# A four-layer graph network on one core: after each gather of the GpSimd queue, 300 bytes of a row of its own are set to zero

## The chip, the cores and the metric

The kernel runs on one core of a Trainium2 chip. The metric is the time on the device in microseconds, the median of several runs; a profiled execution gives the rows that are read below. The five engines have an instruction queue each: TensorE (PE), VectorE (DVE), ScalarE (ACT), GpSimd (POOL) and SyncE (SP). SP does no arithmetic here, it starts DMAs. POOL starts the indirect ones, in which a list of row numbers says which rows of a table in device memory are fetched (a gather) or written (a scatter).

## What is computed

2708 nodes with 128 features each, and a sparse weighted adjacency matrix `adj` of 2708 x 2708 (about 17 entries to a row, the diagonal among them). Four layers follow each other, each `x = layernorm(x + layer(x))`:

```python
x = _layernorm(x + _L0_gnn_ref(x, adj))   # (adj.T @ x) / column sums of adj
x = _layernorm(x + _L1_gnn_ref(x, adj, ...))
#   messages = gelu(s[i] + d[j] + b); aggregated[i] = sum_j adj[i, j] * messages[i, j]
#   h = gelu([x, aggregated] @ upd_w.T + upd_b) + x, then a layernorm with weights
x = _layernorm(x + _L2_gnn_ref(x, adj, ...))
#   adj @ (x @ W) + b, normalised over all nodes, leaky relu
x = _layernorm(x + _L3_gnn_ref(x, adj, ...))
#   4 attention heads: s = exp(8 tanh(leaky_relu(x1[i] + x2[j]) @ a / 8)) * adj, rows normalised,
#   out = leaky_relu(s @ x @ Wlin.T), heads joined by w
```

## The kernel before

The nodes lie in 22 blocks of 128 rows (the last has 20).

**Layer 0 and the search.** SP loads `adj` block by block into a ring of nine buffers (`rows`). For each block PE multiplies it into the sums of layer 0 (L420). POOL clears the block's diagonal in place (`clear_diagonal`, L410); ACT then counts the entries of each row (L431). DVE searches each row for its entries (`extract`: L445, L450, L458 to L488) and keeps up to 32 columns and weights a row. Nodes are ranked by their number of entries (`ranking`), and `place` writes each node's list to its place in a sorted table, `lists_dram`, by scatters of POOL (L255). `layer0` then normalises the sums four blocks at a time (L790, into `dx` or `late`), transposes them, makes `d` of layer 1 from them, has SP store it to `d_dram` (L813), and scatters the rows to `dx_dram` (`own_scatter`). The tile `dx` has two buffers. The search of blocks 13 to 21 and their transposes come after the last L790 by a stated order (`behind`).

**Layer 1.** For each block of 128 sorted nodes `messages` gathers, slot by slot, the row of `d_dram` of the neighbour in that slot: 128 rows of 512 bytes by one indirect DMA of POOL. The slots go in groups of up to eight into one of five buffers `msg`; DVE adds the block's own term to the group (L896), ACT takes the gelu (L899), and DVE weighs each slot into a sum (L882, L884). `update` finishes the block and scatters its rows to `x2_dram`. Meanwhile PE, ACT and SP transpose `adj` into `at_dram` (L969, L974, L976), the first blocks loaded once more.

**Layer 2.** `layer2(k)` gathers the rows of `at_dram` in sorted order into the ring and multiplies (L1018); it begins while layer 1 still runs. Its normalisation follows, with the tables for layer 3.

**Layer 3.** 100 groups of four gathers each from `t2_dram` (`fetch`, into nine buffers `g`), then products on DVE, sums on ACT, and PE.

**What sets the order.** A scheduler that works with modelled durations orders each engine's instructions when the kernel is built, and takes what is ready; in the search and `layer0` the order of DVE is that of the text, and in layer 3 that of PE, DVE and ACT. POOL's order is the scheduler's throughout. Each engine works its queue in order: an instruction that waits holds up all behind it. POOL's queue holds the diagonal clears, all scatters and all gathers. For a tile that is written again the scheduler adds a wait of the later write for the earlier, on POOL itself too.

`gather` is the helper by which layers 1, 2 and 3 fetch rows: 368, 22 and 400 times.

Of the kernel before, what the change touches and what calls it, by code (L numbers as in the profile page):

```python
# [28 lines left out]
I8 = mybir.dt.int8  # L29
# [56 lines left out]
def gnn_resnorm_kernel(  # L86
# [21 lines left out]
    nc = tc.nc  # L108
# [98 lines left out]
    keep = ctx.enter_context(tc.tile_pool(name="keep", bufs=1))  # L207
# [31 lines left out]
    ones = keep.tile([P, P], FP, name="ones")  # L239
    nc.gpsimd.memset(ones, 1.0)  # L240

    def natural(dram, b0, b1):

        return dram[b0 * P : b1 * P, :].rearrange("(b p) w -> p b w", p=P)

    def gather(dst, table, index):
        nc.gpsimd.indirect_dma_start(  # L247
            out=dst,
            out_offset=None,
            in_=table[0:N, :],  # L250
            in_offset=bass.IndirectOffsetOnAxis(ap=index, axis=0),
        )

    def scatter(table, index, rows):
        return nc.gpsimd.indirect_dma_start(  # L255
            out=table,
            out_offset=bass.IndirectOffsetOnAxis(ap=index, axis=0),
            in_=rows,
            in_offset=None,
        ).ins  # L260
# [76 lines left out]
    with ExitStack() as layer:  # L337
# [527 lines left out]
        def messages(b, x_s, three):  # L865
# [24 lines left out]
            for c0, c1 in chunks_of(kk):  # L890
                kc = c1 - c0
                msg = msgs.tile([P, 8, D], FP, name="msg")
                for k in range(kc):
                    gather(msg[0:n, k, :], d_dram, idx[0:n, b, c0 + k + 1 : c0 + k + 2])
                mk = msg[0:n, 0:kc, :]
                nc.vector.tensor_tensor(  # L896
                    mk, mk, s_ps[0:n].unsqueeze(1).to_broadcast((n, kc, D)), ALU.add
                )
                nc.scalar.activation(mk, mk, AF.Gelu)  # L899
                for k in range(kc):  # L900
                    weigh(c0 + k + 1, msg[0:n, k, :])
# [99 lines left out]
        def layer2(k):  # L1001

            b, n = TURNS[k], BLOCKS[TURNS[k]][1]
            at = ring.tile([P, N], FP, name="at_rows", tag="rows")
            gather(at[0:n, :], at_dram, perm[0:n, b : b + 1])
            weighed = small.tile([P, P], FP, name="weighed", bufs=1)
            nc.scalar.activation(
                weighed[0:n], ones[0:n], AF.Copy, scale=column_sum[0:n, b : b + 1]
            )
            for ib in range(NBLK) if k == 0 else ORDER:  # L1010
                i0, m = BLOCKS[ib]
                if ib == 21:

                    nc.tensor.matmul(
                        accs2[5][:, 2 * D : 3 * D], lhsT=weighed[0:n], rhs=xw[0:n, b, :],
                        start=False, stop=False,
                    )
                nc.tensor.matmul(  # L1018
                    accs2[ib // 4][0:m, (ib % 4) * D : (ib % 4 + 1) * D],
                    lhsT=at[0:n, i0 : i0 + m],  # L1020
                    rhs=xw[0:n, b, :],
                    start=(k == 0 and ib % 4 == 0),
                    stop=(k == NBLK - 1 and ib in (3, 7, 11, 15, 19, 20)),
                )
# [73 lines left out]
    with ExitStack() as layer:  # L1098
        work = layer.enter_context(tc.tile_pool(name="bn", bufs=1))
        small = layer.enter_context(tc.tile_pool(name="bn_small", bufs=2))  # L1100
        hb = work.tile([P, NBLK, D], FP, name="hb")
        x2 = work.tile([P, NBLK, D], FP, name="x2")
        nc.sync.dma_start(x2[:, 0:NFULL, :], natural(x2_dram, 0, NFULL))
        nc.sync.dma_start(x2[0:NREM, NFULL, :], x2_dram[NFULL * P : N, :])
        a_all = keep.tile([P, HEADS, D], FP, name="a_all")
# [133 lines left out]
    with ExitStack() as layer:  # L1239
# [290 lines left out]
        def fetch(i):  # L1530
            b, j = quads[i]
            e = BLOCKS3[b][0] * (P // BLOCKS3[b][0])
            g4 = got.tile([P, 4, RW], FP, name="g4")
            for r in range(4):
                ch = CHUNK3[b] + 4 * j + r
                gather(g4[0:e, r, :], t2_dram, idx3[0:e, ch : ch + 1])
            gathered[i] = g4
# [559 lines left out]
```

## Time and profile before

| | |
|---|---|
| three runs, us | 1930.35, 1936.67, 1926.28; median 1930.35 |
| the profiled execution, span | 1936.7 us |
| busy: PE, DVE | 1240.9 us (64%), 1166.6 us (60%) |
| busy: POOL, ACT | 892.8 us (46%), 776.5 us (40%) |
| POOL's gathers of layer 1 (`msg`) | 368, mean 947 ns |
| POOL's gathers of layer 3 (`g`) | 400, mean 996 ns |
| DMA issued by POOL (queue 0) | 190.77 MB in 60496 packets |
| granted clock of PE, mean | 0.667 |

The span is the time from the first to the last instruction of that one execution. A line of the views below names a line of the kernel, the engine, the operation, the tile written and the tiles read, the shapes and how often; then come times. In a view in order of time the first two numbers are the start and the duration in us, and a bracket at the end gives how long the engine was idle before the instruction, and what ended that. In a view of groups the numbers after the bar are the busy time in us, the mean of one in ns, and the idle time before them. "issue" and "remote" stand where the profile names no instruction of another engine that ended the wait. SPq is SP's queue of DMA issues.

### The profile page before, as it was taken

How to read it: one execution, taken by the hardware profiler on the slowest of the kernel's cores; microseconds unless marked ns; L12 is line 12 of the kernel's file. 1: busy time of each engine (PE TensorE's matmuls, PEld its weight loads, DVE VectorE, ACT ScalarE, POOL GpSimd, SP SyncE). 2: the span in 40 equal slices, each digit the busy share in tenths (PEclk: the TensorE clock that was granted, in tenths of full speed). 3: DMA queues.
4: the chain of work that ended last, by engine and by line, in shares of the span. 5: the costliest groups of instructions: out<-in, count | busy, mean ns of one | idle time of the engine just before them, and what ended most of it. 6: DMA issues, size and time to landing. Idle time of an engine off the chain costs nothing. (4 is left out here: it accounts for less than half of the span.)

```text
span 1936.7 us, 23643 instructions
## 1 busy us (share of the span) xinstructions
PE 1240.9 (64%) x5771; PEld 864.1 (45%) x5771; DVE 1166.6 (60%) x4895; ACT 776.5 (40%) x3156; POOL 892.8 (46%) x1003
## 2 busy tenths in 40 slices
PE   7974313353446553554673748888788788878885
PEld 7973212242334442554663314544444444444444
DVE  8997445675635423433447417777678677676774
ACT  3565345543324210211122415555455555445553
POOL 1004654445653366445331474655555556555430
PEclk9986555555555576776676756676676777666675
DMA  8642645666545525223231574865566655756540
GB/s 283 238 150 79 131 140 165 174 183 174 141 103 142 177 43 160 95 92 140 79 113 44 167 239 131 212 190 163 145 196 183 182 166 160 191 150 192 150 115 7
DMA packets 167676, 289.63 MB, mean 150 GB/s; under 512 B 49600, under 2 KB 121502, under 8 KB 160429
## 3 DMA queue, kind: packets, MB, share of 16 engines
q0 software_dynamic: 60496, 190.77, 34.4%
q1 hardware_dynamic: 99489, 92.57, 15.6%
q10 hardware_dynamic: 7544, 4.69, 1.0%
q8 instruction: 48, 0.79, 0.2%
q14 instruction: 99, 0.81, 0.1%
HBM read 242.51 MB, written 45.36 MB: 149 GB/s over the span
## 5 line engine op out<-in xcount | busy, mean ns | idle before, releaser
L247 POOL DMA_INDIRECT g<-t_dram,idx x400 | 398.6, 996 | 316.0 <-issue 178.9
L247 POOL DMA_INDIRECT msg<-d_dram,idx x368 | 348.6, 947 | 260.2 <-issue 164.8
L1389 ACT ACTIVATE sum_junk<-g 126x128 bf16<-126x128 f32 (+3 forms) x1024 | 301.3, 296 | 142.4 <-issue 59.8
L1358 PE MATMUL z<-x,copies 32*126 32x512 f32 (+3 forms) x800 | 221.3, 944 | 65.8 <-DVE g L1555 45.0
L969 PE MATMUL pt_a<-ident,rows 128*128 128x128 f32 (+2 forms) x475 | 114.1, 395 | 144.4 <-ACT at_sb L974 79.5
L1555 DVE TENSOR_TENSOR g<-g,z 126x1536 f32<-126x1536 f32 (+3 forms) x100 | 175.0, 1750 | 44.0 <-DMA g<-t_dram,idx 15.3
L1018 PE MATMUL acc<-x_nat,at_rows 128*128 128x128 f32 (+2 forms) x968 | 160.7, 326 | 52.3 <-DMA at_rows<-at_dram,perm 26.5
L1389 ACT ACTIVATION_READ_ACCUMULATOR sum_junk<-g 126x1 f32 (+3 forms) x1024 | 191.6, 187 | 0.0
L1018 PEld LDWEIGHTS acc<-x_nat,at_rows 128*128 128x128 f32 (+2 forms) x968 | 144.1, 232 | 65.5 <-issue 38.7
L1363 PE MATMUL z<-g,ident 126*126 126x512 f32 (+3 forms) x200 | 169.3, 941 | 0.7 <-issue 0.7
L1435 PE MATMUL po_s<-wm,g 126*128 126x24 f32 (+6 forms) x800 | 128.6, 316 | 58.5 <-DVE wm L1422 56.2
L1435 PEld LDWEIGHTS po_s<-wm,g 126*128 126x128 f32 (+3 forms) x800 | 124.8, 243 | 75.6 <-DVE wm L1422 67.9
L969 PEld LDWEIGHTS pt_a<-ident,rows 128*128 128x128 f32 (+2 forms) x475 | 82.9, 205 | 167.5 <-ACT at_sb L974 92.8
L884 DVE SCALAR_TENSOR_TENSOR own<-msg,ls,own 128x128 f32<-128x128 f32 (+1 forms) x302 | 105.6, 350 | 85.4 <-ACT msg L899 28.5
L1381 DVE SCALAR_TENSOR_TENSOR g<-g,a_ps 126x1536 f32<-126x1536 f32 (+6 forms) x100 | 151.0, 1510 | 0.0
L420 PE MATMUL acc<-x_nat,rows 128*128 128x129 f32 (+3 forms) x1012 | 128.5, 288 | 26.0 <-DMA rows<-in_adj_dram 14.9
L420 PEld LDWEIGHTS acc<-x_nat,rows 128*128 128x128 f32 (+2 forms) x1012 | 123.0, 198 | 31.2 <-DMA rows<-in_adj_dram 16.0
L1358 PEld LDWEIGHTS z<-x,copies 32*126 32x126 f32 (+3 forms) x800 | 67.8, 261 | 100.3 <-issue 46.5
L899 ACT ACTIVATE msg<-msg 128x896 f32<-128x896 f32 (+4 forms) x55 | 50.4, 917 | 132.9 <-DVE msg L896 92.1
L1373 DVE SCALAR_TENSOR_TENSOR g<-z,a 126x128 f32<-126x128 f32 (+3 forms) x400 | 91.9, 285 | 19.5 <-remote 9.2
L445 DVE FIND_INDEX8 ci<-cv,rows 128x8 uint32<-128x247 f32 (+2 forms) x242 | 98.7, 408 | 0.0
L1363 PEld LDWEIGHTS z<-g,ident 126*126 126x126 f32 (+3 forms) x200 | 42.0, 263 | 124.3 <-issue 117.3
(302 smaller groups left out, 2132.2 us busy)
## 6 DMA issues: line engine op xcount, KB each, us to landing
rows<-in_adj_dram SPq DMA_DIRECT2D x34, 1354.0 KB
at_dram<-at_sb SPq DMA_DIRECT2D x105, 256.0 KB
g<-t_dram,idx POOLq DMA_INDIRECT x400
msg<-d_dram,idx POOLq DMA_INDIRECT x368
t_dram<-t_row SPq DMA_DIRECT2D x21, 256.0 KB
x_s<-dx_dram SPq DMA_DIRECT2D x21, 128.0 KB
at_dram<-at_sb SPq DMA_DIRECT2D x21, 64.0 KB
t_dram<-x_nat SPq DMA_DIRECT2D x5, 256.0 KB
```

The costliest lines, as they stand in the source:

```text
L247: nc.gpsimd.indirect_dma_start(out=dst, out_offset=None, in_=table[0:N, :], in_offset=bass.IndirectOffsetOnAxis(ap=index, axis=0),)
L420: nc.tensor.matmul(accs0[k][0:m, c0 : c0 + f1 - f0], lhsT=rows[0:n, j0 : j0 + m], rhs=x_nat[0:n, b, f0:f1], start=k not in started, stop=( ...
L445: nc.vector.max_index(out=ci[0:n, at], in_max=cv[0:n, at], in_values=rows[0:n, c0 : c0 + cw])
L884: nc.vector.scalar_tensor_tensor(to, m, v, last, ALU.mult, ALU.add)
L969: nc.tensor.transpose(pt[0:m, j, 0:n], rows[0:n, c0 : c0 + m], ident[0:n, 0:n])
L1018: nc.tensor.matmul(accs2[ib // 4][0:m, (ib % 4) * D : (ib % 4 + 1) * D], lhsT=at[0:n, i0 : i0 + m], rhs=xw[0:n, b, :], start=(k == 0 and i ...
L1358: nc.tensor.matmul(z3[0:e, r, :] if r < 3 else z1[0:e], lhsT=copies[g][rows, j, :], rhs=own[b][1][rows, :], start=True, stop=r < 3, skip_g ...
L1363: nc.tensor.matmul(z1[0:e], lhsT=ident[0:e, 0:e], rhs=g4[0:e, 3, 0:HD], start=False, stop=True, skip_group_check=True,)
L1381: nc.vector.scalar_tensor_tensor(z, z, 0.0, a_ps[0:e].unsqueeze(1).to_broadcast((e, count, HD)), ALU.max, ALU.mult)
L1389: nc.scalar.activation(junk[0:e], g4[0:e, r, hd * D : (hd + 1) * D], AF.Identity, accum_out=sc[0:e, r, hd : hd + 1],)
L1435: nc.tensor.matmul(po[:, p0 * HEADS : (p0 + g) * HEADS], lhsT=g4s[i][0:e, r, HD : HD + D], rhs=wm[0:e, 4 * i + r, :, :], start=True, stop= ...
L1555: nc.vector.tensor_tensor(z, z, z3[0:e], ALU.add)
```

## The change

A new tile `pause`, one row of 300 int8, is kept for the whole kernel. The helper `gather` sets it to zero on GpSimd after it has issued its DMA. Nothing reads the tile.

```diff
     ones = keep.tile([P, P], FP, name="ones")
     nc.gpsimd.memset(ones, 1.0)
 
+    pause = keep.tile([1, 300], I8, name="pause")
+
     def natural(dram, b0, b1):
 
         return dram[b0 * P : b1 * P, :].rearrange("(b p) w -> p b w", p=P)
@@ -250,6 +252,7 @@
             in_=table[0:N, :],
             in_offset=bass.IndirectOffsetOnAxis(ap=index, axis=0),
         )
+        nc.gpsimd.memset(pause, 0)
 
     def scatter(table, index, rows):
         return nc.gpsimd.indirect_dma_start(
```

## The prediction

> **What bounds the kernel now.** I read first the busy time of each engine in seven stretches of the span, then GpSimd's (POOL's) own instructions in order of time, then who waits for them. The chain of work that ended last is of no use here: it breaks off after four pieces in the last 4 us.
>
> ```profile
> core 0: us, PE busy (x) PEld busy (x) DVE busy (x) ACT busy (x) POOL busy (x), PEclk, DMA share, GB/s
> 0.00:148.00 148.00, 122.01 (x973) 116.70 (x973) 141.29 (x757) 77.36 (x80) 9.64 (x76) 0.94 0.63 224
> 148.00:203.00 55.00, 27.40 (x128) 23.33 (x128) 42.60 (x245) 25.84 (x85) 27.21 (x36) 0.57 0.31 88
> 203.00:325.00 122.00, 26.01 (x120) 19.45 (x118) 50.37 (x220) 49.29 (x78) 69.63 (x74) 0.54 0.53 136
> 325.00:657.00 332.00, 155.06 (x629) 120.02 (x627) 186.09 (x935) 131.04 (x280) 166.31 (x175) 0.55 0.57 151
> 657.00:1024.00 367.00, 207.71 (x1209) 180.12 (x1208) 143.85 (x615) 58.90 (x161) 171.21 (x182) 0.70 0.34 111
> 1117.00:1937.00 820.00, 647.90 (x2512) 369.54 (x2512) 549.88 (x1893) 401.78 (x2384) 422.47 (x424) 0.67 0.57 163
> ```
>
> To 148 us DVE is the bound (141 of 148 busy) and POOL is all but idle (9.6). From 148 to 203 no engine is full: the line runs through POOL's scatters. From 203 to 657 the engines wait for each other. Layer 3 (from 1117) leans on PE, 648 of 820.
>
> ```profile
> 103.59 0.29 POOL L410 TENSOR_SCALAR_AFFINE_SELECT rows<-rows 128x128 f32<-128x128 f32 x1 [4.95 <-PE acc L420]
> 108.82 0.36 POOL L410 TENSOR_SCALAR_AFFINE_SELECT rows<-rows 128x128 f32<-128x128 f32 x1 [4.94 <-DVE ci L445]
> ...
> 148.15 1.15 POOL L255 DMA_INDIRECT lists_dram<-lists,rank  x1 [10.68 <-DVE lists L557]
> 162.86 0.96 POOL L255 DMA_INDIRECT lists_dram<-lists,rank  x1 [5.79 <-DVE deg L720]
> 179.26 0.98 POOL L255 DMA_INDIRECT dx_dram<-dx,rank  x1 [8.13 <-DVE wrong L636]
> 191.93 0.97 POOL L255 DMA_INDIRECT dx_dram<-dx,rank  x1 [2.63 <-issue]
> 202.44 0.99 POOL L247 DMA_INDIRECT msg<-d_dram,idx  x1 [4.48 <-DMA x_s<-dx_dram]
> 203.74 0.95 POOL L247 DMA_INDIRECT msg<-d_dram,idx  x1 [0.30 <-issue]
> ```
>
> The bracket is POOL's idle time before the instruction. The diagonal clears (L410) come every 5.24 us with 4.95 free; then the scatters of lists and of `dx`; then the first gather at 202.44, and 44 gathers without a pause, 1.25 us apart (0.95 busy, 0.30 between). That a late scatter is felt elsewhere at once shows on DVE:
>
> ```profile
> 186.01 1.15 DVE L790 TENSOR_SCALAR dx<-h,sums,var 128x128 f32<-128x128 f32 x4 [6.94 <-DMA dx_dram<-dx,rank]
> ```
>
> `dx` has two buffers; the third group waited 6.94 us until the first group's four scatters had landed. The last stores of `d_dram`, and with them the first gather, hang on that instruction.
>
> **The change, part by part.** Nothing is removed. It adds 790 memsets of 1x300 int8 (`gather` serves layer 2 as well: 368 + 22 + 400). The built order of POOL decides where they go. A memset depends on no gather, only on the memset before it, so the scheduler draws them all forward into what it took for idle time: 355 between the second diagonal clear and the first scatter of lists (18, 14, 15, 14, 14, then twelve runs with 170 in all, then 30, 27, 29, 24), 83 from there to the first gather (25, 16, 15, 1, 12, 14), 315 in 298 to 657 us, 37 ahead of the last scatter of layer 1 at 1024 us, **none in layer 3**. The order of the other POOL instructions differs in a few scatters of lists; on PE, DVE and ACT some transposes and searches of layer 1 change places (166 of 11,919 entries on PE). I price that at nothing, with some 5 us either way in the range.
>
> The length of one. The trace has no int8 memset of this width; its float32 memsets give the scale:
>
> ```profile
> L1287 POOL MEMSET own_x<- 128x768 f32 x1 | 0.7, 738 | 12.9 <-ACT t_row L1227 12.9
> L382 POOL MEMSET caps<- 128x1 f32 x22 | 0.8, 93 | 0.0
> L229 POOL MEMSET lists<- 128x396 f32 x1 | 0.4, 418 | 0.0
> ```
>
> (738 - 93) / 767 = 0.84 ns an element; 93 + 299 x 0.84 = 345 ns for 300 elements. Were four bytes moved as one element it would be 75 of them, 155 ns. The 22 small memsets of L382 follow each other every 0.034 us because they wait for nothing; these wait for POOL's own semaphore, so they can't overlap. The two POOL instructions of the trace that do so start 44 and 62 ns after the one that released them: I add 0.05. That makes 0.395 us; ends 0.2 (packed) and 0.425 (0.363 for the longer uint8 start of 115 ns, plus 0.062). I take 0.395, since the 396-wide row is the nearest.
>
> The Trainium skill, page "VectorE: DVE Perf Modes", section "Zero memsets can be issued as uint32 (trn2)", says of VectorE that a memset costs one cycle per element whatever the type, and that a memset of zero can be reissued over a quarter as many 4-byte words. Read for GpSimd, its first half would give the 0.395 and its second, which fits 300 bytes of zero, the 0.2. No row here decides it.
>
> POOL's lateness, run by run (run x 0.395 against the idle time, less 0.30 ahead of a DMA). To 50 us the 75 memsets take 29.6 us of 31.8 idle: on time. The next 170 take 67.2 of 60.3: 6.9 late at 108.82. Then 110 take 43.5 of 37.8: **12.6 late** at the first scatter of lists. (Those 280 fit only if one takes at most 0.35 us.) The next: 25 take 9.9 of 5.5: 17.0; 16 where there is no gap, 6.3: 23.2; 15 take 5.9 of 7.8: 21.3 at the first `dx` scatter; 13 take 5.1 of 2.3: 24.1; 14 take 5.5 of 4.2: **25.4 late at the first gather**. At 0.2 it would be 0, at 0.425 36.3.
>
> What hides it. The late diagonal clears are covered by DVE: at 11 us a block it is far behind them, and only the count of block 12 (clear at 87.87, about 5 late, plus 2.65 us of ACT at L431) comes near the key at 100.47 that needs it. Without that cover DVE would stall 1 us for each 1 us. The late scatters have no cover: the third `dx` group moves by 21, the stores of `d_dram` behind it too, SP's loads of lists queue behind the load of `ls`, which waits for the scatters, and all gathers stand behind in POOL's queue.
>
> How much of 25.4 reaches the end. The second group of eight gathers is issued by 220 and its add on DVE runs only at 242.79, DVE having been slow meanwhile (below). If DVE is as slow at the same hour, data landing at 223 + 25 = 248 costs 5.6; if the slow stretch moves with the gathers, all 25.4. I take 16, about the middle. The 315 memsets in 298 to 657 I put at nothing: gathers wait 164.6 us there for one of five buffers (`msg`, 18.12 us the longest), so a gather issued 10 to 20 late still lands ahead of its use. Uncovered, they would add what doesn't fit, 30 us at most. The 37 at 1024 need 14.6 of 16.23 idle. Sum: span 1936.7 + 16 = 1953. That execution was the slowest of three runs (1926.28 to 1936.67), so against the median: 1930.35 + 16 = **1946 us**.
>
> A rule speaks against the change beyond that. The Trainium skill, page "SBUF — State Buffer", section "SBUF: two separate sides", says that GpSimd and some forms of VectorE share a port pair under a lock, one blocking the other for a whole instruction. The 22 L790 instructions (346 ns) are of a form that it names; by an estimate from it each would wait up to one memset, 22 x 0.345 = 7.6 us, and the sum would be 1954. Before, L790 ran 0.33 to 0.36 beside POOL's DMAs but for a few, which shows no such loss.
>
> **The rivals.** *Hidden* (0.2): a memset takes 0.2 to 0.3, POOL is 0 to 5 us late at 203, the time stays at 1930. For it: type and width are not in the trace. Against it: every POOL memset row scales with elements.
>
> *Faster* (0.2): the slow stretch shrinks. From 200 to 330 us DVE waits 63 us, and mostly for its own last instruction:
>
> ```profile
> 222.46 0.36 DVE L884 SCALAR_TENSOR_TENSOR own<-msg,ls,own 128x128 f32<-128x128 f32 x1 [4.50 <-issue]
> 226.69 0.36 DVE L884 SCALAR_TENSOR_TENSOR own<-msg,ls,own 128x128 f32<-128x128 f32 x1 [3.56 <-remote]
> 213.17 38.54 SPq L976 DMA_DIRECT2D at_dram<-at_sb  x7
> ```
>
> The last line is SP's queue: seven stores spread over 38.5 us in the same stretch as the 44 gathers. If the gathers come 25 us later than the stores, the two no longer meet, and half of 63 is saved: 1930 + 16 - 32 = 1914. It turns the sign when more than 16 of the 63 go. Against it: the stores hang on the same late DVE instructions (their transposes are issued behind the last L790), so both may move together.
>
> *All of it* (0.1): 25 in full and the 30 of layer 1 uncovered: 1930 + 55 = 1985. That the memsets spread through layer 3 as the words of the change suggest (400 x 0.395 = 158 us more on POOL, 422 of 820 busy) the built order rules out.
>
> **How the numbers follow.** The forecast has 0.5, all of it 0.1: slower 0.6. Hidden 0.2, faster 0.2. About 0.5% (9.7 us) is what a measurement of this kernel tells from no change. The range goes from the faster rival, 1914, less than a tenth below it, to 1984; the forecast's own is 1936 to 1956.
>
> **What would show it.** Right: memset rows of about 345 ns, about 0.40 apart in a run; the first scatter of lists at about 161, the third `dx` group at 207, the first gather at 228; layer 3's 820 us as before. Wrong: memsets of 0.2 or less; a first gather before 210; or a first gather at 228 and a last scatter of layer 1 at 1024 all the same, which would mean that layer 1 takes it all up.

## The result: 28 us slower, and where they arise

The changed kernel took 1956.49 us (median of four runs, 1952.8 to 1957.91), the kernel before 1928.32 (median of four, 1924.44 to 1936.67). The ratio is 1.0134, 95% interval 1.0106 to 1.0163, that is 20 to 31 us more. The profiled execution took 1957.8 us, its span is 1956.1.

In the changed kernel the gather is L249, the memset L255, the scatter L258, and lines further down have moved by three. POOL's instructions in order of time:

```profile
12.27 7.05 POOL L255 MEMSET pause<- 1x300 int8 x18
...
148.27 9.60 POOL L255 MEMSET pause<- 1x300 int8 x24
158.06 1.14 POOL L258 DMA_INDIRECT lists_dram<-lists,rank  x1 [0.19 <-issue]
...
198.30 0.99 POOL L258 DMA_INDIRECT dx_dram<-dx,rank  x1 [0.40 <-issue]
...
219.78 5.47 POOL L255 MEMSET pause<- 1x300 int8 x14
226.23 0.98 POOL L249 DMA_INDIRECT msg<-d_dram,idx  x1 [0.97 <-DMA x_s<-dx_dram]
```

Eighteen memsets take 7.05 us: (7.05 - 0.34) / 17 = 0.395 us from one to the next. The scatter of lists stood at 148.15 after 10.68 us of idle time; now it stands at 158.06 right behind memsets. The first scatter of `dx` moved from 179.26 to 198.30 (19.0), the first gather from 202.44 to 226.23 (23.8). VectorE in order of time, the third `dx` group and the second group of gathered rows (242.79 before):

```profile
204.87 1.12 DVE L793 TENSOR_SCALAR dx<-h,sums,var 128x128 f32<-128x128 f32 x4 [11.52 <-DMA dx_dram<-dx,rank]
...
254.65 1.22 DVE L899 TENSOR_TENSOR msg<-msg,own 128x1024 f32<-128x1024 f32 x1 [2.08 <-remote]
```

The wait for the first group's scatters has grown from 6.94 to 11.52 us, and the group itself is 18.9 late. The busy time of the engines by stretch:

```profile
core 0: us, PE busy (x) PEld busy (x) DVE busy (x) ACT busy (x) POOL busy (x), PEclk, DMA share, GB/s
0.00:148.00 148.00, 121.09 (x972) 115.67 (x972) 139.42 (x749) 73.39 (x78) 119.52 (x406) 0.95 0.63 224
203.00:325.00 122.00, 39.23 (x157) 30.65 (x157) 52.62 (x236) 45.94 (x77) 85.51 (x112) 0.51 0.51 136
325.00:657.00 332.00, 155.66 (x632) 123.21 (x632) 190.75 (x965) 135.89 (x285) 254.70 (x452) 0.53 0.57 153
657.00:1024.00 367.00, 192.47 (x1123) 168.23 (x1123) 135.44 (x585) 56.95 (x154) 187.10 (x216) 0.68 0.33 108
1117.00:1937.00 820.00, 653.77 (x2558) 370.01 (x2558) 557.10 (x1938) 409.23 (x2401) 426.47 (x430) 0.69 0.59 168
```

To 148 us POOL's 9.64 busy us have become 119.52, and DVE has lost 2 (141.29 to 139.42). From 325 to 657 POOL does 88 us more (166.31 to 254.70), while PE, DVE and ACT do within 5 us what they did before. In layer 3 POOL does what it did.

Lateness against the trace of before: first gather 23.8, first scatter of layer 1's result 21.8, the sixth 36.8, the eleventh 23.7, the last 31.7, first gather of layer 3 28.2, end 19.4 (the profiled execution of before was the slowest of its runs; the medians differ by 28). So it arises before the first gather, grows and shrinks again within layer 1, and stays.

The gathers of layer 1 as a group, of before and then of after (the number behind the second bar is the idle time ahead of them, and behind it stands what ended most of that):

```profile
L247 POOL DMA_INDIRECT msg<-d_dram,idx x368 | 348.6, 947 | 260.2 <-issue 164.8 <-ACT at_sb L974 74.6 <-ACT junk L948 13.3
```

```profile
L249 POOL DMA_INDIRECT msg<-d_dram,idx x368 | 348.3, 946 | 150.6 <-issue 138.7 <-ACT ln_junk L306 4.5 <-ACT at_sb L977 3.7
L255 POOL MEMSET pause<- 1x300 int8 x790 | 267.5, 339 | 42.0
```

Between two DMA issues of POOL lie 0.30 us even when nothing is waited for. For 368 gathers that is 110 us, so the real room before was 260.2 - 110 = 150 us. The 315 memsets of layer 1 need 315 x 0.395 = 124. Most of the room was used, and no more: of the 150.6 us of idle time after, 40 are more than the gaps.

### The profile page after: what moved, and what is told of

Same layout as the page of the kernel before. It is cut to its first block, busy times and chain, and to the rows that moved or that the text cites. A ratio compares the mean times of both kernels' runs of the same rounds, so it can differ in the third digit from the quotient of the medians.

```text
span 1956.1 us, 24437 instructions
## 1 busy us (share of the span) xinstructions
PE 1235.0 (63%) x5771; PEld 864.3 (44%) x5771; DVE 1166.3 (60%) x4895; ACT 774.6 (40%) x3156; POOL 1158.2 (59%) x1793
## 5 line engine op out<-in xcount | busy, mean ns | idle before, releaser
L249 POOL DMA_INDIRECT g<-t_dram,idx x400 | 398.6, 996 | 307.1 <-issue 169.3
L249 POOL DMA_INDIRECT msg<-d_dram,idx x368 | 348.3, 946 | 150.6 <-issue 138.7
L255 POOL MEMSET pause<- 1x300 int8 x790 | 267.5, 339 | 42.0
L972 PE MATMUL pt_a<-ident,rows 128*128 128x128 f32 (+2 forms) x475 | 118.3, 410 | 191.7 <-ACT at_sb L977 144.6
L1021 PE MATMUL acc<-x_nat,at_rows 128*128 128x128 f32 (+2 forms) x968 | 164.6, 332 | 66.7 <-DMA at_rows<-at_dram,perm 39.4
L972 PEld LDWEIGHTS pt_a<-ident,rows 128*128 128x128 f32 (+2 forms) x475 | 86.9, 212 | 214.8 <-ACT at_sb L977 154.2
L977 ACT COPY at_sb<-pt_a 128x512 f32<-128x512 f32 (+3 forms) x154 | 67.6, 475 | 81.5 <-DMA at_dram<-at_sb 78.5
```

Source lines behind the costliest of these rows:

```text
L249: nc.gpsimd.indirect_dma_start(out=dst, out_offset=None, in_=table[0:N, :], in_offset=bass.IndirectOffsetOnAxis(ap=index, axis=0),)
L255: nc.gpsimd.memset(pause, 0)
L972: nc.tensor.transpose(pt[0:m, j, 0:n], rows[0:n, c0 : c0 + m], ident[0:n, 0:n])
L1021: nc.tensor.matmul(accs2[ib // 4][0:m, (ib % 4) * D : (ib % 4 + 1) * D], lhsT=at[0:n, i0 : i0 + m], rhs=xw[0:n, b, :], start=(k == 0 and i ...
```

## The experiments

The chips that the runs fell on are of two kinds: on some the kernel before takes about 1930 us, as in the runs above, on others about 1605. Each chip was used in one set of runs only, so whether a chip stays of its kind is not shown. Each ratio below compares runs on one chip. Microseconds are the ratio less 1, times the median of before on that chip.

"Theory" below is that POOL is late at the scatters and the first gather, because memsets of later gathers were drawn forward, and that this is carried to the end. The rival holds that each memset costs something wherever it stands, by sharing the engine or SBUF.

**First set of runs, on a 1605 chip (before 1606.77).** `inplace` ties each memset behind its gather, so that none is drawn forward:

```diff
-        nc.gpsimd.indirect_dma_start(
+        did = nc.gpsimd.indirect_dma_start(
...
-        nc.gpsimd.memset(pause, 0)
+        with tc.issue_after(did.ins):
+            nc.gpsimd.memset(pause, 0)
```

> All 790 memsets stay, each behind its own gather, none ahead of the first gather. Lateness theory (what costs is GpSimd coming late to the lists scatters, the dx scatters and the first gather, because memsets of later gathers were drawn ahead of them): first lists scatter at 148 us and first gather at 202 us as in the kernel before; the 40 gathers that fill the first five msg buffers are 0.395 us further apart, which is 3 us for the first group of 8 and 16 us for the fifth, later hidden behind the wait for buffers; so 1928 to 1945 us, most likely 1931. Rival 'every memset costs' (GpSimd's 312 us of memsets cost 28 us wherever they stand, by sharing SBUF with VectorE): about 1956 us, as the changed kernel.

`first355` and `first438` issue a memset only behind the first so many gathers, counted in a list; `first400` only behind those of layer 3, by `if table is t2_dram:`.

```diff
+        paused.append(1)
+        if len(paused) <= 438:
-        nc.gpsimd.memset(pause, 0)
+            nc.gpsimd.memset(pause, 0)
```

> Memsets after the first 355 gathers only; all 355 are then ahead of the first lists scatter, as in the changed kernel, and none behind it. Lateness theory: the first lists scatter is 9.9 us late as in the changed kernel (158 us), but with no memset between the lists scatters and the first gather GpSimd is level again by the first dx scatter (179 us), the first gather stands at 202 us, and the time is that of the kernel before, 1928 us within 4. Rival 'every memset costs': 355/790 of 28 us, 1941 us. Rival 'the lists are the path' (the loss comes from the late lists scatters): some 10 us, 1938 us.

> Memsets after the 400 gathers of layer 3 only; 355 of them are ahead of the first lists scatter, 25 among the lists scatters, 20 between these and the first dx scatter, none later, none in layer 1. Lateness theory: 10 us late at the first lists scatter, about 15 at the first dx scatter, about 10 at the first gather (212 us), carried at one to one to the end: 1938 us (1935 to 1943). Rival 'every memset costs': 400/790 of 28 us, 1942 us, which lies too near to tell; the place of the first gather and the distance from there to the end tell more than the time.

> Memsets after the first 438 gathers only; these stand where the changed kernel has its first 438, all ahead of the first gather, and the 352 inside layer 1 are gone. Lateness theory: first lists scatter at 158, first gather at 226 us, both as in the changed kernel; from there on a shift of 22 to 24 us of everything and no further growth: 1952 us (1948 to 1957). If the 352 memsets in layer 1 cost by themselves too, it is well below that; rival 'every memset costs': 438/790 of 28 us, 1944 us.

| kernel | first lists scatter | first gather | ratio | us |
|---|---|---|---|---|
| before (trace of the second set) | 147.9 | 200.8 | | |
| first355 | 158.0 | 206.6 | 1.0024 [1.0001, 1.0046] | +4 |
| first400 | 158.8 | 217.8 | 1.0081 [1.0054, 1.0107] | +13 |
| first438 | 158.6 | 226.8 | 1.0131 [1.0097, 1.0164] | +21 |
| inplace | 148.2 | 201.9 | 1.041 [1.0384, 1.0436] | +66 |

The first three follow the theory: the same lateness of 10 us at the lists costs 4, 13 or 21 us, depending on how much of it is still there at the first gather (5.8, 17.0, 26.0). Two of my figures were off: I had POOL level again by 179 us in `first355` (it is 5 late there), and only 10 late at the first gather in `first400`. The rival's 13, 14 and 16 us, which were shares of the 28 us of the other kind of chip, fall with the first of them.

A second rival is that the memsets change the order in which the scheduler lets the other engines work. By the traces, `first355` has VectorE and PE in the very order of before; `first400` and `first438` (and the changed kernel, but for some 50 places) have VectorE in another order in some 800 places of layer 1, and both in the same. From `first400` to `first438` the order stays but for two places each on ACT and POOL, the first gather comes 9.0 us later, and the time is 8 us longer (the intervals overlap a little). So on this kind of chip lateness costs by itself, without another order. Against the trace of before the last results of layer 1 come 12.8, 21.6 and 34.6 us late, more than the first gathers; layer 3 gives 2 to 6 us of it back. The traces are of two chips, so these few us are not explained.

`inplace` was a plain miss: 1928 to 1945 us was written for a chip of 1930, where before takes 1607 here, but a loss of 66 us with nothing drawn forward fits no account of lateness, and the rival's even price of 28 not either. POOL in order of time:

```profile
235.19 0.95 POOL L249 DMA_INDIRECT msg<-d_dram,idx  x1 [0.16 <-issue]
236.14 0.34 POOL L256 MEMSET pause<- 1x300 int8 x1
236.64 0.95 POOL L249 DMA_INDIRECT msg<-d_dram,idx  x1 [0.16 <-issue]
237.59 0.34 POOL L256 MEMSET pause<- 1x300 int8 x1
```

A gather and its memset take 1.45 us (0.95 + 0.34 + 0.16) against 1.25 for a gather alone (0.95 + 0.30): the memset is partly hidden in the gap between two DMA issues and costs 0.20, not 0.395. That it is felt at all suggests that on this chip gathers set the pace of layer 1; `inplace` alone does not show it, for its VectorE too works in another order (368 places). To the last scatter of layer 1 the kernel falls 61.9 us behind (817.8 to 879.7), for 390 gathers x 0.20 = 78; layer 3 adds 7 for 400 (700.3 to 707.3 from its first gather to the end). A second theory had to be set beside the first: two costs, the lateness ahead of the first gather, and POOL's time inside layer 1 where its gathers set the pace.

**Second set, on another 1605 chip (before 1603.51).** The changed kernel and the kernel before themselves, and two tests of the lateness. `late60` has 60 memsets in a row between the last of the first thirteen `dx` scatters and the first gather (each gather of layer 1 ordered behind them), and none elsewhere; `three_dx` has no memset and one more `dx` buffer:

```diff
-            h = brief.tile([P, 4, D], FP, name="h0", bufs=5)
+            h = brief.tile([P, 4, D], FP, name="h0", bufs=3)
...
-                dx = brief.tile([P, count, DX], FP, name=f"dx{count}", bufs=2)
+                dx = brief.tile([P, count, DX], FP, name=f"dx{count}", bufs=3)
```

> The changed kernel itself, once more, beside the other kernels of this call. Lateness theory: first gather at 226 us, from there a shift to the end of 0.87 to 1 times that lateness, as with the first 438 memsets alone (ratio 1.013), plus little for the 352 memsets in layer 1 where GpSimd issues gathers back to back every 1.25 us: these are 0.395 us each, and if none is hidden they add up to 139 us, if all are hidden 0. By the first run of the change (ratio 1.0134, of a longer time): 1.013 to 1.020. A ratio over 1.03 says that the memsets in layer 1 cost by themselves where gathers set the pace.

> The kernel before, once more, for a trace beside the other kernels of this call. First lists scatter 148, first gather 202 us; gathers of layer 1 1.25 us apart; time as the runs of the kernel before on the same chip.

> No memset behind any gather; instead 60 in a row between the last of the 13 dx scatters and the first gather. The diagonal clears, lists scatters, dx scatters and the third dx group of VectorE stand as before (third group at 186 us); only the gathers come late: 60 x 0.395 = 23.7 us from 198 on, first gather at 222 us, 19 us late. Lateness theory, with the first gather as the place where it counts: the end 17 to 20 us late, ratio 1.011. Rival (VectorE's third dx group and the stores behind it are the path, the gathers have room): under 5 us, ratio below 1.003.

> The kernel before, without any memset, with three dx buffers instead of two (and three h buffers instead of five, to make the room). The third dx group no longer waits for the landing of the first dx scatters (186 us, it can run from about 178). GpSimd's 13 dx scatters can then follow each other at 1.27 us from 179 to 195. Lateness theory with the opposite sign: first gather 4 to 7 us earlier than 202, and the end earlier by as much: ratio 0.996 to 0.997. Rival (the start of the gathers is not what the end hangs on): ratio 1.000. A different order of the other engines, which the new buffers bring, can cost or gain some us besides.

`before_again`, one run, took 1602.05 us, with the first lists scatter at 147.9 and the first gather at 200.8. `again`: ratio 1.0759 [1.072, 1.0799], 122 us, far from the 1.013 to 1.020 that the lateness theory gave and beyond the 1.03 that was to speak for a cost inside layer 1. The same change costs four times as much on this kind of chip. The first gather is 24.8 late, the eleventh scatter of layer 1 124, the last 123, the end 123: all the rest is lost between the first gather and the eleventh scatter, where 315 memsets stand. The gather group, by the trace of before on this chip and then of the changed kernel:

```profile
L247 POOL DMA_INDIRECT msg<-d_dram,idx x368 | 348.3, 947 | 137.0 <-issue 103.5 <-ACT at_sb L974 14.9 <-DVE kb L488 3.7
```

```profile
L249 POOL DMA_INDIRECT msg<-d_dram,idx x368 | 348.4, 947 | 121.7 <-issue 102.1 <-ACT msg L902 3.7 <-ACT x_st L874 3.0
```

Less the 110 us of gaps the room is 137 - 110 = 27 us here, not 150. Of 124 us of memsets 97 don't fit. Measured from the first to the 224th gather: 366.4 us before, 465.8 after, 99.4 more.

`late60` came between the two accounts: ratio 1.0051 [1.0023, 1.0078], 8 us, for a first gather 21.0 late. Its rows stand where they were meant to:

```profile
196.25 0.96 POOL L265 DMA_INDIRECT dx_dram<-late,rank  x1 [0.30 <-issue]
197.21 23.65 POOL L255 MEMSET pause<- 1x300 int8 x60
221.83 0.98 POOL L257 DMA_INDIRECT msg<-d_dram,idx  x1 [0.98 <-DVE cv L460]
```

VectorE's third `dx` group was on time there (185.3), and with it the search of blocks 13 to 21, which stands behind it. Late gathers alone cost some 0.4 of their lateness; `first438`, where both are late, 0.8. But the scheduler also gave layer 1 another order (224 gathers in 360.3 us, 6 fewer), so the split between the two is not shown. The first result of layer 1 was 22.8 late, so late gathers do reach the results; the gain of 15 us came between the thirteenth result (32.5 late) and the fourteenth (17.1).

`three_dx` showed the first step and failed in the end: ratio 1.0047 [1.0022, 1.0072], 8 us slower. The third `dx` group ran without a wait and the first gather 4.4 us earlier (200.8 to 196.4):

```profile
177.14 1.12 DVE L790 TENSOR_SCALAR dx<-h,sums,var 128x128 f32<-128x128 f32 x4
```

Yet the 224 gathers took 382.0 us instead of 366.4. The new buffers changed the order of DVE, ACT, PE and SP in layer 1. Which of these costs the 16 us stays open; as a test of what an earlier first gather is worth it decides nothing.

**Third set: the complement of `first438`.** It fell on a 1930 chip (before 1931.79).

```diff
+        paused.append(did.ins)
+        if len(paused) > 438:
+            with tc.issue_after(paused[0]):
-        nc.gpsimd.memset(pause, 0)
+                nc.gpsimd.memset(pause, 0)
```

`issue_after(paused[0])` holds these memsets behind the first gather, so that none moves ahead of it.

> The complement of the kernel with the first 438 memsets: memsets only behind gathers 439 and later, none of them ahead of the first gather, 323 inside layer 1 and 29 before its last scatter, in runs much like the changed kernel's. Up to the fourteenth gather after the first 52 everything stands as before: first gather at 201 us. Theory 'two costs' (lateness before the first gather, plus GpSimd's time inside layer 1 wherever gathers set its pace): on a chip that runs the kernel before in some 1605 us, the x_n scatters fall behind from the second on, by about 100 us at the tenth, and stay so: 1605 + 95 = 1700 us (1685 to 1715), ratio 1.06. On a chip that runs the kernel before in some 1930 us: ratio 1.000 to 1.005. Rival 'the two only cost together' (the memsets in layer 1 only tip over a pace that the late start has already upset): under 30 us, ratio below 1.02.

> The changed kernel itself beside the kernel with memsets 439 and later alone, on one chip. Theory 'two costs': 24 us more than that kernel; on a chip that runs the kernel before in some 1605 us, ratio 1.07 to 1.08, on one of some 1930 us, ratio 1.013.

`rest352`: ratio 1.0004 [0.9979, 1.0029]. Of the 352 memsets nothing is felt at the end on this chip; inside layer 1 the results run up to 19.5 us late against the trace of before (the sixth) and are 8.4 ahead at the eleventh. `again_2`: 1.015 [1.012, 1.0181], 29 us, as in the first measurement, and 33 us above `rest352` by the medians, where 24 were expected. So on such a chip the loss hangs on the 438 ahead of the first gather. Whether they do it by lateness alone was not run there: `rest352` has VectorE, ACT and PE in the order of before, the changed kernel has not, and the two were told apart only on a 1605 chip (above).

**Fourth set, on a 1605 chip again (before 1609.53).** The same kernel and `inplace` once more.

> The kernel with memsets behind gathers 439 and later alone, once more, for a chip of the other kind if this is one. Theory 'two costs': where the kernel before takes some 1605 us, 95 us more (ratio 1.06); where it takes some 1930 us, nothing (1.000) as in the first run of it. Rival 'the two only cost together': ratio below 1.02 on both.

> All 790 memsets behind their own gathers, none drawn forward, once more. On a chip of some 1605 us as in its first run, ratio 1.04: gathers 1.45 instead of 1.25 us apart where they set the pace. On a chip of some 1930 us theory 'two costs' has neither lateness before the first gather nor a pace set by gathers: the first five groups of gathers come 1.6 to 8 us later, the rest is covered by GpSimd's idle time, ratio 1.000 to 1.004.

`rest352_2`: ratio 1.053 [1.0498, 1.0563], 85 us, with the first gather at 202.2 (200.8 in the trace of before) and VectorE, ACT and PE in the order of before. So these 85 us come from the memsets and not from another order of these engines, and the two costs do not need each other. `inplace_2`: 1.0402 [1.0374, 1.0431], as the first time. What `inplace` costs on a 1930 chip was not measured. POOL of `rest352_2` in order of time, and below it a line from DVE's waits in 203 to 660 us (us in total, times, longest), first of before on a 1605 chip, then of `rest352_2`:

```profile
345.51 0.94 POOL L250 DMA_INDIRECT msg<-d_dram,idx  x1 [0.30 <-issue]
346.45 9.42 POOL L259 MEMSET pause<- 1x300 int8 x24
356.26 0.95 POOL L250 DMA_INDIRECT msg<-d_dram,idx  x1 [0.39 <-ACT x_nt L946]
```

```profile
DVE msg L896 <- DMA msg<-d_dram,idx: 22.3, 5, 9.3
```

```profile
DVE msg L903 <- DMA msg<-d_dram,idx: 56.1, 11, 11.8
```

The scheduler put 24 memsets where it took POOL for idle; on the chip the next gather came 9.5 us later than the 1.25 us pace had it, and DVE waited for gathered rows eleven times instead of five.

All traces in one measure, the us from the first to the 224th gather (the memsets among them in brackets):

| | before | memsets inside layer 1 | first438 | inplace |
|---|---|---|---|---|
| 1930 chips | 480.2 (0) | 480.1, 480.8 (315), 472.2 (323) | not run | not run |
| 1605 chips | 366.4 (0) | 465.8 (315), 458.3 (323) | 374.5 (0) | 399.1, 403.8 (217) |

With 315 or 323 memsets drawn into layer 1 both kinds of chip need 458 to 481 us, without any in it 360 to 382 or 480. On a 1605 chip the queue of POOL sets the pace, and memsets push it up to where a 1930 chip is anyway, for a reason of its own.

Where it is felt shows on DVE's waits from 203 to 325 us, of before on the 1930 chip of the prediction, then on a 1605 chip:

```profile
DVE own L884 <- remote: 14.0, 5, 3.6
DVE kb L474 <- issue: 9.5, 2, 5.8
```

```profile
DVE own L884 <- ACT msg L899: 16.4, 2, 15.4
DVE msg L896 <- DMA msg<-d_dram,idx: 13.0, 4, 9.0
```

On the second DVE waits for named work, for ACT and for gathered rows, and is busy 82.00 of these 122 us. On the first it is busy 50.37 and its waits end with no instruction of another engine. Counted over the trace, waits of over 0.4 us in which DVE waits only for its own semaphore sum to 106 us for before on the 1930 chip, 84 for the changed kernel, 93 for `rest352`; on the 1605 chips there is none but one of 1.4 us in `three_dx`. DVE is not alone in this: over the trace of before on the 1930 chip the waits that end with "remote" come to 230.5 us on DVE and 241.6 on ACT (159.6 and 200.1 for the changed kernel), and in none of the ten traces of 1605 chips does a wait of either end so. The waits for DVE's own semaphore are only a part of the some 325 us between the kinds: layer 3, longer by 119 us, has two of them, 1.7 us. Why some chips do this no run here shows.

## Why the prediction was right, and where it was off

The time, 1946, is 10 us short, just beyond the forecast's own 1936 to 1956 and inside the range; the sign and the mechanism ahead of the first gather hold. That the run fell on a chip of the 1930 kind was luck: on the other kind the same sum would have been some 100 us short, for there its term of nothing for layer 1 measured 85. Step by step:

- **Length of a memset, 0.395 us.** Measured 339 ns for one (345 said) and 0.395 from one to the next. The packed end of 0.2 is out: 300 bytes of zero are not written as 75 words on GpSimd, which the section "Zero memsets can be issued as uint32 (trn2)" of the Trainium skill's page "VectorE: DVE Perf Modes" did not promise either. With it falls the rival *Hidden*.
- **Lateness, 12.6, 21.3 and 25.4.** Measured 9.9, 19.0 and 23.8; the third `dx` group at 204.9 (207 said), the first gather at 226.2 (228). The 2.7 us that are missing at the lists are in the joints: a clear and fourteen memsets follow each other every 5.67 us, not every 0.29 + 14 x 0.395 = 5.82, and there are some twenty such runs. The first run stands behind the first clear of the trace, not behind the second.
- **Late diagonal clears are covered by DVE.** DVE lost 2 us of work to 148 us; `first355`, which has all 355 early memsets, costs 4 us on a 1605 chip, and these go with the 5 us that POOL was still late at the `dx` scatters.
- **The port lock**, which the page "SBUF — State Buffer" of the Trainium skill, section "SBUF: two separate sides", speaks for: the median of L790 was 343 and 347 ns for its two tiles, that of L793 (the same line after) is 347 and 345; the 13 of the 22 beside which a memset ran have 347, the nine others 344. VectorE shows no sign of the 7.6 us. The memsets do: 14 of the 790 took more than 350 ns (355 to 458), and each of the 14 overlapped a tensor_scalar or a cast of VectorE (117 memsets did), seven of them an L793; none of the 673 others took more than 350. It comes to 0.9 us in all. `again` has 17 such memsets, all beside the same kinds of instruction.
- **The carry: "Of 25.4 I take 16, about the middle" is the term that was mis-sized.** It measured 26 to 29 (ratios 1.0134 and 1.015), the whole lateness of 23.8 and a little more; in it is whatever the other order of layer 1 costs, which I had put at nothing and which no run on this kind of chip takes apart. My ends were a slow stretch of DVE that keeps its hour, or that moves with the gathers. By the second group it looked like the middle: its add moved by 11.9 us, the gathers by 23.8. But the stretch moved along: DVE's waits for its own semaphore were 24 us in 200 to 250 and 48 in 250 to 350 before, and are 5 and 56 after (12 us fewer in sum), and at the first result of layer 1 the lateness was 21.8 again. One early instruction told too little.
- **The 315 memsets of layer 1 at nothing.** Right for the chip of the prediction (`rest352`, 1.0004), by a reading that was too loose. I took 164.6 us as waits for buffers. It is all the idle time ahead of the 156 gathers from 320 to 660 us:

```profile
L247 POOL DMA_INDIRECT msg<-d_dram,idx x156 | 148.4, 951 | 164.6 <-issue 75.0 <-ACT at_sb L974 74.6 <-ACT junk L948 13.3
```

Of it 156 x 0.30 = 47 us are the gaps between two issues, and the view names no reader of a `msg` buffer. The 118 us that are left are a little less than the 124 that the memsets need; over all 368 gathers the room is 260.2 - 110 = 150. It fitted, but narrowly. On a 1605 chip it gives 27 us of room, and the bound of "30 us at most" uncovered is wrong there by some 60.

- **The 37 at 1024 at nothing.** The last two scatters of layer 1 lie 17.7 us apart, 17.2 before.
- ***Faster*** fell: the stores and the gathers moved together, as its own counter-argument said (the seven stores from 213.17 to 233.90, the first gather from 202.44 to 226.23). On a 1605 chip the same seven stores (211.69) meet the same gathers and DVE has no wait of over 0.4 us for its own semaphore there, so their meeting is not what makes the slow stretch. ***All of it*** fell at 1930 us, but came true, and more, where the kernel takes 1605: 122 us. The parts measured alone, 21 and 85, leave some 16 of these unaccounted for, on three different chips.

## What to carry to other kernels

A cheap instruction that depends on nothing is not executed where it is written: a scheduler with modelled durations draws it forward into what it takes for idle time, here 438 of 790 ahead of the first gather, and a price that is a few hundredths of a microsecond too low makes the queue late: the 280 that were put into the last gaps ahead of the lists fit them at 0.35 us each and took 0.395. Before counting idle time of a DMA-issuing queue as room, subtract the gap that lies between any two issues; what is left was 150 us on one chip and 27 on another. A test of such a change tells most where the other engines keep their order, as in `first355` and `rest352`, and little where they do not, as in `late60` and `three_dx`. And a price measured on one chip holds for its bound alone: the same edit cost 1.3% where the pace came from elsewhere and 7.6% where this queue set it.

## What was unexpected on the hardware

- Chips of one type ran the unchanged kernel in 1603 to 1610 us or in 1928 to 1932 us, at a mean granted clock of 0.69 to 0.72 against 0.66 to 0.68. To the first gather both are alike (200.8 and 202.4 us); layer 1 takes 617 and 822 us from there, layer 3 700 and 819.
- A memset of 0.34 us behind a DMA issue adds only 0.20 us to the queue: the gap to the next issue shrinks from 0.30 to 0.16 us.
- A memset on GpSimd beside a tensor_scalar or a cast of VectorE took up to 458 ns instead of 338, in 14 of 117 such meetings; none of the 673 other memsets took more than 350 ns.
